# A cross-attention kernel on one core: the output projection as seven block products, weights divided early, statistics on ScalarE

## The chip, the core and the metric

The kernel runs on one core of a Trainium2 chip. The core's engines work side by side, each through its own queue in order: TensorE (PE in the profile, PEld for its weight loads) multiplies and writes its results to PSUM, eight banks of 512 fp32 columns each; VectorE (DVE), ScalarE (ACT) and GpSimd (POOL) do elementwise work; SyncE (SP) issues the transfers (DMA) between device memory and SBUF. In this kernel only VectorE and ScalarE read PSUM. Times are device microseconds; the kernel's time is the median of several runs.

## The reference

For each of 64 batches, with `x` of 256 rows by 512 and `c` (the context) of 256 rows by 384, all fp32:

```python
text_p  = x @ W_text + b_text           # 256 x 512
audio_p = c @ W_audio + b_audio         # 256 x 512
Q = layer_norm(text_p, g1, beta1)
K = layer_norm(audio_p, g2, beta2)
alpha = softmax(Q @ K.T / sqrt(512))    # 256 x 256
H = (alpha @ audio_p) @ W_out + b_out
out = layer_norm(H + x, g_out, beta_out)
```

## The kernel before

There is one loop over batches `b`, and it is a pipeline over four of them: iteration `b` computes the scores of batch `b`, the context and output products of `b-1` (called `last`), the end of the output of `b-2` (called `done`), q and k of `b+2`, and turns x and c of `b+3`. The order of the work is written out by hand, call by call; the pools say when a buffer comes free, and every engine runs its own calls in the order written.

*q and k* (class `Blocks`). A product of 256 rows by 512 columns is cut in a two by two grid of blocks and computed with seven block products instead of eight (a scheme of Strassen's kind). `sum_x` and `sum_c` form the sums of the turned x and c on GpSimd, `weight_sums` those of the weights, once. `products` writes two of the seven products (256 columns each) to one bank of PSUM, and takes four banks in all; `leave(n)` adds product n into the rows on VectorE, so there are seven such steps for each of q and k: three of 512 columns (1, 6 and 7, where one product is broadcast to both halves) and four of 256. For c, with three chunks of 128 in the contraction, it takes 11 matmuls of 256 columns; for x, with four, 14.

*Norms of q and k.* The weights are centred beforehand, so the mean is zero; `square` sums the squares on ScalarE, `rstd_of` forms the reciprocal root on GpSimd, `normalise` scales on ScalarE. The rows are then stored to device memory (`store`) and read back in another order (`fetch`), `turn` transposes them in blocks of 32 by 32 on VectorE, and `affine` applies gamma and beta on ScalarE. The same way round through memory is taken by the exponentials (`store_e`, `fetch_e`, `turn_e`).

*Attention.* `scores` (8 matmuls of 256 columns), `maxima` on VectorE, `exponentials` on ScalarE with their row sums, `reciprocals` on VectorE. `context` multiplies the turned exponentials with c itself (not with the projected c) and copies the result z to SBUF. W_audio and W_out are folded into one matrix `wao` in the beginning, and both biases into `bao`; `multiply(t)` therefore needs three matmuls of 512 columns for each of two row tiles.

*Output.* `add_bias` adds `bao` to x on GpSimd. `evict(t)` multiplies the product with the reciprocal of the row sum and adds x, on VectorE; then bn_stats and bn_aggr give mean and variance, GpSimd the reciprocal root, and `shift` and `settle` on VectorE apply the norm. The rows go to device memory.

*What sets the order around the change.* PSUM has three pools: four banks in a ring for q and k, two for scores and context, two for the output. On VectorE an iteration begins with `done`'s second eviction, statistics and shift, then `last`'s turned exponentials, then the maxima, and ends with the turn of x and c of `b+3` and `last`'s first eviction. On SP the store of the exponentials stands ahead of the reads of q and k; then come the reads of the exponentials, the loads of x and c and the stores of out, q and k.

Of the kernel before, what the change touches and what calls it, by code (L numbers as in the profile page):

```python
# [9 lines left out]
F32 = mybir.dt.float32  # L10
AF = mybir.ActivationFunctionType
# [11 lines left out]
def kernel(  # L23
# [37 lines left out]

    nc = tc.nc
    ctx.enter_context(tc.manual_schedule())
    B, L, D = x.shape
# [10 lines left out]
    work = ctx.enter_context(tc.tile_pool(name="work", bufs=2))  # L77
    small = ctx.enter_context(tc.tile_pool(name="small", bufs=4))
    scratch = ctx.enter_context(tc.tile_pool(name="scratch", bufs=3, space=bass.MemoryType.DRAM))
    p_pj = ctx.enter_context(tc.tile_pool(name="p_pj", bufs=4, space=PSUM))  # L80
    p_at = ctx.enter_context(tc.tile_pool(name="p_at", bufs=2, space=PSUM))
    p_y = ctx.enter_context(tc.tile_pool(name="p_y", bufs=2, space=PSUM))

    def squares(dst, src):

# [73 lines left out]
    def arrange(dst, rows_sb, chunks, copy):  # L159

        copy(
            dst.rearrange("p k (q i) -> p k q i", q=NQ),
            rows_sb.rearrange("p (q k i) -> p k q i", q=NQ, i=SQ),
        )

    class RowTurn:


        def __init__(self, rows_sb, chunks, name):
            self.rows, self.chunks = rows_sb, chunks  # L170
            tag = "y" if chunks == DC else "kT"
            self.ar = work.tile([P, 2, chunks, P], F32, tag=tag, name=f"{name}r")
            self.T = work.tile([P, chunks, 2 * P], F32, tag=name, name=f"{name}_0")

# [8 lines left out]
    def turn_weights():  # L183

        waT = []
        for k in range(HC):
            if k % 2 == 0:
                half = work.tile([P, 2, DA], F32, tag="zT", name=f"waT_{k}")
            waT.append(half[:, k % 2, :])
            ps = p_at.tile([P, AC, P], F32, tag="at", name="ps_wa")  # L190
            for a in range(AC):
                nc.tensor.transpose(ps[:, a, :], war[:, a, k, :], ident)
            nc.scalar.copy(
                waT[k].rearrange("p (q a i) -> p a q i", q=NQ, i=SQ),
                ps.rearrange("p a (q i) -> p a q i", q=NQ),
            )
        return waT
# [13 lines left out]

    def fold_multiply(a):

        ps = ps_wao[a] = p_y.tile([P, D], F32, tag="y", name="ps_wao")
        for k in range(HC):
            nc.tensor.matmul(
                ps,
                lhsT=waT[k][:, bass.ts(a, P)],
                rhs=wo_sb[:, k, :],
                start=(k == 0),  # L220
                stop=(k == HC - 1),
            )
# [59 lines left out]
        }  # L282
        return {p: [ap[:, k, :] for k in range(n)] for p, ap in ss.items()}

    def sum_c(cT):

        part = lambda i, j: cT[:, j, bass.ts(i, P)]
        s = work.tile([P, 5, P], F32, tag="csum", name="csum")
        add = nc.gpsimd.tensor_tensor
        add(s[:, 0], part(1, 0), part(1, 1), ALU.add)  # L290
        add(s[:, 1], s[:, 0], part(0, 0), ALU.subtract)
        add(s[:, 2:4], cT[:, 0:3:2, :P], cT[:, 0:3:2, P:], ALU.subtract)
        add(s[:, 4], part(0, 1), s[:, 1], ALU.subtract)
        return {
            1: [part(0, 0)], 2: [part(0, 1), part(0, 2)], 4: [part(1, 1), part(1, 2)],
            5: [s[:, 0], part(1, 2)], 6: [s[:, 1]], 7: [s[:, 2]], 3: [s[:, 4], s[:, 3]],
        }

    def rstd_of(var, n):
        ve = small.tile([P, n], F32, tag="ve", name="ve")  # L300
        nc.gpsimd.tensor_scalar(ve, var, EPS, None, ALU.add)  # L301
        r = small.tile([P, n], F32, tag="rstd", name="rstd")
        nc.gpsimd.tensor_tensor(r, ve, nhalf[:, :n], ALU.pow)  # L303
        return [r[:, t : t + 1] for t in range(n)]
# [153 lines left out]
    class Attention:  # L458
# [36 lines left out]
        def reciprocals(self):  # L495
            self.rden = small.tile([P, LT], F32, tag="rden", name="rden")
            nc.vector.reciprocal(self.rden, self.den)

        def store_e(self):
            self.d = scratch.tile([L, S], F32, tag="ed", name=f"ed_{self.b}")  # L500
            nc.sync.dma_start(self.d.rearrange("(t p) s -> p t s", p=P), self.e)
# [21 lines left out]
        def context(self):  # L523
# [3 lines left out]
            for lo in range(0, AC, 2):  # L527
# [10 lines left out]
                        )  # L538
                nc.scalar.copy(self.zT[:, lo : lo + n, :], ps[:, :n, :])

        def start_output(self):
            self.y = work.tile([P, LT, H], F32, tag="y", name=f"y_{self.b}")
            self.mv = small.tile([P, LT, 2], F32, tag="mvy", name="mvy")
            self.ps_y = {}

        def multiply(self, t):
            ps = self.ps_y[t] = p_y.tile([P, D], F32, tag="y", name="ps_y")
            for k in range(AC):
                nc.tensor.matmul(  # L549
                    ps,  # L550
                    lhsT=self.zT[:, k, bass.ts(t, P)],
                    rhs=wao_sb[:, k, :],
                    start=(k == 0),
                    stop=(k == AC - 1),
                )
# [13 lines left out]
            self.r = {lo + t: r for t, r in enumerate(rstd_of(self.mv[:, lo : lo + n, 1], n))}  # L569

        def shift(self, t):
            nc.vector.scalar_tensor_tensor(
                self.y[:, t, :], self.y[:, t, :], self.mv[:, t, 0:1], go_sb, ALU.subtract, ALU.mult
            )

        def settle(self, t):
            nc.vector.scalar_tensor_tensor(  # L577
# [40 lines left out]
    k[0].multiply(1)  # L618
    mean_wa = means(wa_sb, AC, "mwa")
    k[0].evict(0)  # L620
    war = blk.tile([P, AC, HC, P], F32, tag="kq", name="war")
    for a in range(AC):
        arrange(war[:, a], wa_sb[:, a, :], HC, nc.gpsimd.tensor_copy)
    x_turn.tile(0)
    x_turn.tile(1)
    k[0].evict(1)
# [4 lines left out]
    bt_row = bt_sb.rearrange("p (o h) -> p o h", o=1)  # L631
    mean_ba = means(ba_row, 1, "mba")
    centre(wa_sb, mean_wa, AC)
    wa_blocks = weight_sums(wa_sb, 1, "wasum")
    for n, k2 in ((2, 0), (3, 1), (5, 1), (4, 0)):
        wa_blocks[n].append(wa_sb[:, 2, k2 * H2 : (k2 + 1) * H2])
    k[0].normalise()
    k[0].store()
    wo_sb = weight_by_square(w_out, HC, "wo", nc.sync)
# [69 lines left out]
    fold_multiply(2)  # L709
    fold_evict(2)  # L710
    bao_sb = fold_bias(part)
    q[1].normalise()
    q[1].store()
    q[1].fetch()
# [4 lines left out]
    for b in range(B - 2):  # L719
        three = b + 3 < B  # L720
        at = Attention(b)
        at.scores()
        if done:
            done.evict(1)
            done.scales()
            done.shift(0)
        if last:
            last.turn_e()
        at.maxima()
        if done:  # L730
            done.shift(1)
        at.exponentials()
        at.store_e()
        if b:
            q[b + 1].fetch()
            k[b + 1].fetch()
        at.fetch_e()
        if b + 4 < B:
            blocks[b + 4] = load_squares(b + 4)
        rows[b + 1] = load_rows(b + 1)  # L740
        q2 = q[b + 2] = Blocks("q", b + 2, xs.pop(b + 2), wt_blocks, bt_sb)
        q2.products(1, 2)
        q2.leave(1)
        if done:
            done.settle(0)
        q2.products(6, 5)
        q2.leave(6)
        q2.leave(2)
        q2.leave(5)
        q2.products(7, 3)  # L750
        q2.leave(3)
        q2.leave(7)
        q2.products(4)
        q2.leave(4)
        q2.square()
        q[b + 1].turn()
        at.reciprocals()
        if last:
            last.context()
        q[b + 1].affine(g1_sb, be1_sb)  # L760
        if done:
            done.settle(1)
            done.store()
        q2.scales()
        add_bias(b)
        k[b + 1].turn()
        k[b + 1].affine(g2_sb, be2_sb)
        q2.normalise()
        q2.store()
        k2 = k[b + 2] = Blocks("k", b + 2, cs.pop(b + 2), wa_blocks, ba_sb)  # L770
        k2.products(1, 2)
        k2.leave(1)
        k2.products(6, 5)
        k2.leave(6)
        k2.leave(2)
        k2.leave(5)
        k2.products(7, 3)
        k2.leave(3)
        k2.leave(7)
        k2.products(4)  # L780
        k2.leave(4)
        k2.square()
        k2.scales()
        if last:
            last.start_output()
            last.multiply(0)
        if three:
            xT[b + 3] = turn_x(b + 3)
            xs[b + 3] = sum_x(xT.pop(b + 3))
            cT[b + 3] = turn_c(b + 3)  # L790
            cs[b + 3] = sum_c(cT.pop(b + 3))
        k2.normalise()
        k2.store()
        if last:
            last.evict(0)
            last.multiply(1)
        done, last = last, at


# [2 lines left out]
    k[B - 1].fetch()  # L802
    rows[B - 1] = load_rows(B - 1)
    at.scores()
    done.evict(1)
    done.scales()
    last.turn_e()
    at.maxima()
    at.exponentials()
    add_bias(B - 2)  # L810
    last.context()
    at.reciprocals()
    q[B - 1].turn()
    last.start_output()
    last.multiply(0)
    q[B - 1].affine(g1_sb, be1_sb)
    at.transpose_e()
    at.copy_e()
    done.finish()
    done.store()  # L820
    last.evict(0)
    last.multiply(1)
    k[B - 1].turn()
    k[B - 1].affine(g2_sb, be2_sb)
    add_bias(B - 1)
    at.context()
    last.evict(1)
    last.scales()
    end = Attention(B - 1)
    end.scores(end=True)  # L830
    at.start_output()
    at.multiply(0)
    end.maxima()
    end.exponentials()
    end.reciprocals()
# [50 lines left out]
```

## Time and profile before

| what | us |
|---|---|
| median of 3 runs | 1449.62 (1448.57 to 1450.06) |
| the profiled execution's own time | 1451.83 |
| its span, first to last instruction | 1450.0 |
| TensorE busy | 1429.6 (99%) |
| VectorE busy | 1223.8 (84%) |
| ScalarE busy | 731.0 (50%) |
| GpSimd busy | 699.0 (48%) |
| DMA engines, mean busy share | about 0.8 |

Busy time is a share of the whole span, and an engine with less than the most of it can still set the time for a stretch. A group of the profile is read as: line, engine, operation, output and inputs, shape and count, then busy time and the mean of one in ns, then the idle time just before it and what ended it. A matmul shows as two records of its kind. The chain that ended last is followed back from the end through whatever released each step.

### The profile page before, as it was taken

To read this page: it belongs to the slowest core of one execution; us is meant where nothing else is said; L and a number is where in the kernel's file an instruction comes from. 1 tells how busy PE (TensorE), PEld (TensorE's weight loads), DVE (VectorE), ACT (ScalarE), POOL (GpSimd) and SP (SyncE) were. 2 spreads that over 40 slices of the span, in tenths; PEclk is the share of its full clock that TensorE was granted. 3 is DMA by queue.
4 is the path that set the end of the run, shared out by engine and by line. 5 is a ranking of instruction groups with operands and counts; after the bars stand their busy time and mean duration, and the time that the engine had idled before them with its cause. 6 is when DMAs were issued, how large, how long until landed. Compare 5 with 4: busy or idle time off the path is not lost.

```text
span 1450.0 us, 20424 instructions
## 1 busy us (share of the span) xinstructions
PE 1429.6 (99%) x5799; PEld 1098.4 (76%) x5799; DVE 1223.8 (84%) x2061; ACT 731.0 (50%) x1689; POOL 699.0 (48%) x1041
## 2 busy tenths in 40 slices
PE   7999999999999999999999999999999999999997
PEld 4777787787787787787777777877877877877874
DVE  5669988888888888888888889888888888888876
ACT  4545554554544544545545545545545445455452
POOL 5445545544545444455445445445444544454442
PEclk9999999999999999999999999999999999999999
DMA  9678878887877978887888878778778788878872
GB/s 206 171 226 248 244 209 245 234 217 229 246 209 229 236 211 237 217 237 229 222 233 235 216 232 242 210 231 246 200 237 228 223 229 224 230 229 233 222 205 89
DMA packets 450275, 322.41 MB, mean 222 GB/s; under 512 B 154740, under 2 KB 382580, under 8 KB 450164
## 3 DMA queue, kind: packets, MB, share of 16 engines
q1 hardware_dynamic: 450164, 321.11, 79.4%
q8 instruction: 47, 0.77, 0.2%
q14 instruction: 64, 0.52, 0.1%
HBM read 204.09 MB, written 116.92 MB: 221 GB/s over the span
## 4 chain that ended last, share of the span: by engine, by line
PE 92%; DMA 4%; DVE 1%; SPq 1%; issue 1%; POOL 0%; ACT 0%; POOLq 0%; DVEq 0%
PE ps_q L431 25%; PE ps_y L549 22%; PE ps_k L431 20%; PE ps_sc L470 15%; PE ps_z L532 11%; DMA qd<-qr 1%; DMA cq<-in_ctx_dram 1%; SPq L88 1%; DMA wt<-in_L_xattn_W_text_dram 1%; DMA ed<-e 0%; DMA wo<-in_L_xattn_W_out_dram 0%; DVE kr L442 0%; DVE qr L442 0%; DMA kq<-kd 0%; DVE y L577 0%
## 5 line engine op out<-in xcount | busy, mean ns | idle before, releaser
L301 POOL TENSOR_SCALAR ve<-var 128x2 f32<-128x2 f32 x126 | 27.7, 220 | 675.0 <-ACT junk L339 674.9
L549 PE MATMUL ps_y<-wao,zT 128*128 128x512 f32 x768 | 340.3, 592 | 0.0
L549 PEld LDWEIGHTS ps_y<-wao,zT 128*128 128x128 f32 x768 | 145.8, 190 | 156.1 <-issue 139.2
L470 PEld LDWEIGHTS ps_sc<-kT,qT 128*128 128x128 f32 x1024 | 193.9, 190 | 54.9 <-issue 21.0
L470 PE MATMUL ps_sc<-kT,qT 128*128 128x256 f32 x1024 | 232.0, 380 | 0.6 <-ACT kT L405 0.6
L442 DVE TENSOR_TENSOR qr<-ps_q,qr 128x512 f32<-128x512 f32 x378 | 188.2, 512 | 48.6 <-PE ps_q L431 36.6
L339 ACT ACTIVATE junk<-qr 128x512 f32<-128x512 f32 x126 | 79.4, 630 | 271.5 <-DVE qr L442 271.5
L442 DVE TENSOR_TENSOR kr<-ps_k,kr 128x512 f32<-128x512 f32 x378 | 188.3, 512 | 27.2 <-PE ps_k L431 4.9
L487 ACT ACTIVATE e<-ps_sc,nmx 128x256 f32<-128x256 f32 x128 | 59.4, 469 | 282.5 <-DVE nmx L480 282.5
L532 PE MATMUL ps_z<-eT,c 128*128 128x256 f32 x768 | 176.6, 379 | 0.8 <-ACT eT L521 0.7
L431 PE MATMUL ps_q<-wtsum,xsum 128*128 128x256 f32 x756 | 173.7, 379 | 0.9 <-POOL xsum L276 0.9
L605 POOL TENSOR_TENSOR x<-x,bao 128x512 f32<-128x512 f32 x128 | 171.7, 1362 | 4.0 <-DMA x<-in_x_dram 4.0
L431 PE MATMUL ps_k<-wa,cT 128*128 128x256 f32 x630 | 166.9, 379 | 0.1
L532 PEld LDWEIGHTS ps_z<-eT,c 128*128 128x128 f32 x768 | 145.8, 190 | 21.6 <-ACT eT L521 0.9
L431 PEld LDWEIGHTS ps_q<-wtsum,xsum 128*128 128x128 f32 x756 | 143.5, 190 | 21.1 <-POOL xsum L276 1.7
L303 POOL TENSOR_TENSOR rstd<-ve,nhalf 128x2 f32<-128x2 f32 (+1 forms) x193 | 141.8, 734 | 16.0
L405 ACT ACTIVATE kT<-kT,columns 128x256 f32<-128x256 f32 x256 | 132.4, 588 | 12.7 <-DVE kT L398 10.1
L405 ACT ACTIVATE qT<-qT,columns 128x256 f32<-128x256 f32 x256 | 132.9, 591 | 11.6 <-DVE qT L91 11.5
L431 PEld LDWEIGHTS ps_k<-wa,cT 128*128 128x128 f32 x630 | 119.5, 190 | 16.6 <-PE ps_z L532 0.4
L367 ACT ACTIVATE kr<-kr,rstd 128x512 f32<-128x512 f32 x126 | 84.1, 714 | 74.8 <-POOL rstd L303 74.8
L431 PE MATMUL ps_q<-wt,xT 128*128 128x256 f32 x504 | 119.2, 379 | 0.7 <-DVE xT L91 0.7
L577 DVE SCALAR_TENSOR_TENSOR y<-y,rstd,beo 128x512 f32<-128x512 f32 x128 | 103.6, 810 | 4.9 <-POOL rstd L303 4.6
(113 smaller groups left out, 2204.9 us busy)
## 6 DMA issues: line engine op xcount, KB each, us to landing
x<-in_x_dram SPq DMA_DIRECT2D x64, 512.0 KB, 4.7
kd<-kr SPq DMA_DIRECT2D x64, 512.0 KB, 4.6
kq<-kd SPq DMA_DIRECT2D x256, 128.0 KB, 3.4
qd<-qr SPq DMA_DIRECT2D x64, 512.0 KB, 7.3
qq<-qd SPq DMA_DIRECT2D x256, 128.0 KB, 2.8
xq<-in_x_dram SPq DMA_DIRECT2D x252, 128.0 KB, 2.8
out_dram<-y SPq DMA_DIRECT2D x63, 512.0 KB, 6.4
cq<-in_ctx_dram SPq DMA_DIRECT2D x252, 96.0 KB, 2.5
```

What stands on the lines that cost most here:

```text
L303: nc.gpsimd.tensor_tensor(r, ve, nhalf[:, :n], ALU.pow)
L339: nc.scalar.activation(junk, self.rows[:, t, :], AF.Square, scale=1.0 / math.sqrt(H), accum_out=self.var[:, t : t + 1],)
L367: nc.scalar.mul(row, row, self.r[t])
L405: nc.scalar.activation(self.T[:, k, :], self.T[:, k, :], AF.Identity, bias=bet[:, k : k + 1], scale=gam[:, k : k + 1],)
L431: nc.tensor.matmul(bank[:, j, :], lhsT=side, rhs=w, start=(i == 0), stop=(i == len(pairs) - 1))
L442: add = lambda o, i0, i1: nc.vector.tensor_tensor(o, i0, i1, ALU.add)
L470: nc.tensor.matmul(self.sc[:, t, :], lhsT=self.qT[:, k, bass.ts(t, P)], rhs=self.kT[:, k, :], start=(k == 0), stop=(k == HC - 1),)
L487: nc.scalar.activation(self.e[:, t, :], self.sc[:, t, :], AF.Exp, bias=self.nmx[:, t : t + 1], accum_out=self.den[:, t : t + 1],)
L532: nc.tensor.matmul(ps[:, j, :], lhsT=self.c_sb[:, s, bass.ts(lo + j, P)], rhs=self.eT[:, s, :], start=(s == 0), stop=(s == ST - 1),)
L549: nc.tensor.matmul(ps, lhsT=self.zT[:, k, bass.ts(t, P)], rhs=wao_sb[:, k, :], start=(k == 0), stop=(k == AC - 1),)
L577: nc.vector.scalar_tensor_tensor(self.y[:, t, :], self.y[:, t, :], self.r[t], beo_sb, ALU.mult, ALU.add)
L605: nc.gpsimd.tensor_tensor(xb[:, t, :], xb[:, t, :], bao_sb, ALU.add)
```

## The change

- The output projection of `last` becomes `Blocks` as well: `sum_c(zT)` on GpSimd forms the sums of z (tile `zsum`), `weights_of_three` those of `wao`, once; its seven products are multiplied at the end of the iteration. Leaves 1, 6, 2 and 5 follow in that iteration, 3, 7 and 4 in the next, after the scores. The rows begin with `bao`.
- A block product mixes rows, so the division by the row sum can no longer be done at the end: `divide_e` multiplies the exponentials with the reciprocals on ScalarE before they are stored.
- x is added by `add_x` on GpSimd, in place of `add_bias` (the last two batches keep `add_bias` and the old output).
- `statistics` replaces bn_stats and bn_aggr: on ScalarE, one pass over each row tile for minus the mean, one for the sum of squares around it.
- q, k and the output share one ring of six PSUM banks.
- The order changes: turn and sums of x and c for `b+3` now follow the scores; the reads of q and k stand ahead of the store of the exponentials, which waits for the division, and the loads of the squares of x and c stand ahead of the reads of the exponentials; `reciprocals` follows q's first leave; both shifts and both settles stand between q's turn and k's products.
- In the start, the rearranged copy of W_audio lies in other buffers.

```diff
-    p_pj = ctx.enter_context(tc.tile_pool(name="p_pj", bufs=4, space=PSUM))
+    p_pj = ctx.enter_context(tc.tile_pool(name="p_pj", bufs=6, space=PSUM))
     p_at = ctx.enter_context(tc.tile_pool(name="p_at", bufs=2, space=PSUM))
-    p_y = ctx.enter_context(tc.tile_pool(name="p_y", bufs=2, space=PSUM))
...
+    def weights_of_three(w_sb, name):
+        ws = weight_sums(w_sb, 1, name)
+        for n, k2 in ((2, 0), (3, 1), (5, 1), (4, 0)):
+            ws[n].append(w_sb[:, 2, k2 * H2 : (k2 + 1) * H2])
+        return ws
...
+        def divide_e(self):
+            for t in range(LT):
+                nc.scalar.mul(self.e[:, t, :], self.e[:, t, :], self.rden[:, t : t + 1])
...
+        def start_products(self):
+            self.o = Blocks("y", self.b, sum_c(self.zT, "zsum"), wao_blocks, bao_sb)
+            self.y = self.o.rows
+        def add_x(self):
+            for t in range(LT):
+                nc.gpsimd.tensor_tensor(self.y[:, t, :], self.y[:, t, :], self.xb[:, t, :], ALU.add)
+        def statistics(self):
+            self.nm = small.tile([P, LT], F32, tag="nm", name="nm")
+            self.ssq = small.tile([P, LT], F32, tag="ssq", name="ssq")
+            for t in range(LT):
...
+                nc.scalar.activation(
+                    junk, self.y[:, t, :], AF.Identity, scale=-1.0 / D, accum_out=self.nm[:, t : t + 1]
+                )
+            for t in range(LT):
...
+                nc.scalar.activation(
+                    junk,
+                    self.y[:, t, :],
+                    AF.Square,
+                    bias=self.nm[:, t : t + 1],
+                    accum_out=self.ssq[:, t : t + 1],
+                )
+            self.r = dict(enumerate(rstd_of(self.ssq, LT, total=True)))
...
         at.scores()
         if done:
-            done.evict(1)
-            done.scales()
-            done.shift(0)
+            done.o.leave(3)
+            done.o.leave(7)
+            done.o.leave(4)
+            done.add_x()
         if last:
             last.turn_e()
+        if three:
+            xT[b + 3] = turn_x(b + 3)
+            xs[b + 3] = sum_x(xT.pop(b + 3))
+            cT[b + 3] = turn_c(b + 3)
+            cs[b + 3] = sum_c(cT.pop(b + 3))
         at.maxima()
-        if done:
-            done.shift(1)
         at.exponentials()
-        at.store_e()
+        q2 = q[b + 2] = Blocks("q", b + 2, xs.pop(b + 2), wt_blocks, bt_sb)
+        q2.products(1, 2)
+        q2.leave(1)
+        at.reciprocals()
+        at.divide_e()
         if b:
             q[b + 1].fetch()
             k[b + 1].fetch()
-        at.fetch_e()
+        at.store_e()
         if b + 4 < B:
             blocks[b + 4] = load_squares(b + 4)
+        at.fetch_e()
         rows[b + 1] = load_rows(b + 1)
...
         if done:
-            done.settle(0)
+            done.statistics()
...
         q2.square()
+        q2.scales()
         q[b + 1].turn()
-        at.reciprocals()
+        if done:
+            done.shift(0)
+            done.shift(1)
         if last:
             last.context()
         q[b + 1].affine(g1_sb, be1_sb)
+        k[b + 1].turn()
+        k[b + 1].affine(g2_sb, be2_sb)
         if done:
+            done.settle(0)
             done.settle(1)
             done.store()
-        q2.scales()
-        add_bias(b)
-        k[b + 1].turn()
-        k[b + 1].affine(g2_sb, be2_sb)
         q2.normalise()
         q2.store()
+        if last:
+            last.start_products()
...
-        if last:
-            last.start_output()
-            last.multiply(0)
-        if three:
-            xT[b + 3] = turn_x(b + 3)
-            xs[b + 3] = sum_x(xT.pop(b + 3))
-            cT[b + 3] = turn_c(b + 3)
-            cs[b + 3] = sum_c(cT.pop(b + 3))
         k2.normalise()
         k2.store()
         if last:
-            last.evict(0)
-            last.multiply(1)
+            last.o.products(1, 2)
+            last.o.leave(1)
+            last.o.products(6, 5)
+            last.o.leave(6)
+            last.o.leave(2)
+            last.o.leave(5)
+            last.o.products(7, 3)
+            last.o.products(4)
```

In the ending, batch 61's output is `Blocks` too, its products after the transposition of batch 62's exponentials; batch 60's `statistics` follow the context of 61 and batch 61's follow the last scores; `end` and `at` keep `multiply` and `evict`.

## The prediction

> **What bounds the kernel now.** I read the page's engine shares first, then the chain that ended last, then the costliest groups with shapes kept apart, one line's durations, the DMA issues, and the timeline of two iterations from 616 us on.
>
> The page (busy time, and the chain by engine):
>
> ```profile
> PE 1429.6 (99%) x5799; PEld 1098.4 (76%) x5799; DVE 1223.8 (84%) x2061; ACT 731.0 (50%) x1689; POOL 699.0 (48%) x1041
> ...
> PE 92%; DMA 4%; DVE 1%; SPq 1%; issue 1%; POOL 0%; ACT 0%; POOLq 0%; DVEq 0%
> ```
>
> The chain in the middle (start, length, what):
>
> ```profile
> 616.97 3.45 PE ps_sc L470 x16
> 620.42 6.04 PE ps_q L431 x28
> 626.47 2.59 PE ps_z L532 x12
> 629.05 4.75 PE ps_k L431 x22
> 633.80 5.15 PE ps_y L549 x12
> 638.95 3.45 PE ps_sc L470 x16
> ```
>
> The chain is TensorE alone and has no gap: one iteration (one batch) is 3.45+6.04+2.59+4.75+5.15 = 21.98 us, and in the stretch 200 to 1380 us TensorE is busy in all of it, at a granted clock of 1.00. So a saving on TensorE counts 1:1 as long as no other engine needs more than the new period. A matmul leaves two records (12 for the six y matmuls). A 256-column record costs 215.8 ns (4.75/22), a 512-column one 429.2 ns (5.15/12).
>
> The groups that give my prices (mean ns after the comma), and one line's min/median/max:
>
> ```profile
> L577 DVE SCALAR_TENSOR_TENSOR y<-y,rstd,beo 128x512 f32<-128x512 f32 x128 | 103.6, 810 | 4.9 <-POOL rstd L303 4.6
> ...
> L442 DVE TENSOR_TENSOR kr<-ps_k,kr 128x256 f32<-128x256 f32 x252 | 101.2, 422 | 15.2
> ...
> L558 DVE SCALAR_TENSOR_TENSOR y<-ps_y,rden,x 128x512 f32<-128x512 f32 x128 | 93.1, 728 | 16.3 <-PE ps_y L549 15.6
> L238 DVE BATCH_NORM_STATS2 st<-y 128x6 f32<-128x512 f32 x128 | 88.9, 695 | 4.4
> L442 DVE TENSOR_TENSOR kr<-ps_k,kr 128x512 f32<-128x512 f32 x126 | 87.2, 692 | 12.0 <-PE ps_k L431 4.9
> ...
> L398 DVE STREAM_TRANSPOSE kT<-kq 128x512 f32<-128x512 f32 x124 | 80.8, 689 | 24.0 <-DMA kq<-kd 20.8 <-issue 3.2
> ```
> ```profile
> L577 DVE SCALAR_TENSOR_TENSOR y<-y,rstd,beo x128: 727/743/1846, 99.2 to 1446.2; 128x512 f32<-128x512 f32 x128
> ```
>
> VectorE is the second load: in one period (597.99 to 619.98) it is busy 19.1 us, ScalarE 11.4, GpSimd 11.0; it also waits at times for a DMA (kT). These issues matter later (KB each, median us to landing):
>
> ```profile
> kd<-kr SPq DMA_DIRECT2D x64, 512.0 KB, 4.6
> kq<-kd SPq DMA_DIRECT2D x256, 128.0 KB, 3.4
> qd<-qr SPq DMA_DIRECT2D x64, 512.0 KB, 7.3
> ```
>
> **TensorE.** The six 512-column matmuls of the output become 11 of 256 columns (the shape of k's products): 22 x 215.8 ns = 4.75 us for 5.15, so -0.405 us, and a period of 21.58. In the loop the products stand 61 times: 61 x 0.405 = -24.7 us, and once in the ending: -0.4.
> Against it speaks the Trainium skill ("TensorE: Matmul & The Clock Gate", Back-to-back issue gap): in a stream of weight loads and matmuls the spacing is set by both, so ten more loads per iteration would not be free. A load here is 190 ns; exposed, ten cost +1.9 us and the time would be 1450 - 25 + 116 = 1541. The row decides: k's 22 records carry one load each and still follow at 215.8 ns, so the loads fit beneath. I take -0.405.
>
> **VectorE.** Out go two evictions, two bn_stats, two aggregations; in come seven leaves (three of 512, four of 256). Rows overlap slightly, so I price by spacing from start to start on the timeline: eviction 0.75, bn_stats 0.73, aggregation 0.1, together 3.15; seven leaves 3.75 (0.7, 2 x 0.73, 4 x 0.39). Net +0.6. The rest per iteration: q and k leaves 7.5, transposes 5.05 (eT 0.63, xT 1.16, cT 0.86, qT 1.17, kT 1.23), maxima 0.6, shifts and settles 2.85. In all 19.8 us of 21.58.
> Now the order, from the scores' start as 0, each piece waiting for the later of its input and the queue. The seven leaves of k end at 19.6; the output's first four follow to 21.8, its last three (3, 7, 4) to 1.75 of the next iteration; eT, xT, cT to 4.4; maxima 5.0; leave 1 of q 5.65. There the reciprocal is a new wait: it needs both exponentials of ScalarE, 1.85 after the maxima's start (timeline: 664.43 to 666.3), so 6.25; behind it are six leaves of q. But leave 6 needs TensorE's second pair, ready at 7.15. So VectorE meets TensorE with 0.85 us to spare; then q's leaves end at 10.4, qT 11.6, shifts 13.0, kT 14.2, settles 15.7, k's leaves 19.6 again. Nothing of the net +0.6 reaches the end while that 0.85 lasts; without it each further 0.1 us is 6.1 us of time. Where VectorE is late, TensorE is not stopped at once: with six banks in the ring, output bank (7,3) is the one k's (1,2) filled, free at 17.4 and wanted at 19.4.
>
> **The shared port.** The Trainium skill ("SBUF — State Buffer", Who interferes with whom) calls the second port pair of VectorE and GpSimd an exclusive lock for the whole instruction; VectorE takes it with two SBUF inputs. Shift and settle are such, and the change puts four GpSimd sums near the settles. By that rule four operations could each be blocked for a GpSimd instruction (0.45 to 1.04 us, say 0.75): +3.0 us, period 23.7, and 1450 + 61 x 1.7 = 1554. The row shows a lock (median 743, worst 1846) but a mean of only 810, with the bias additions of 1.36 us beside it then. I take +0.07 each, +0.3 in all, and leave 0.55 us spare.
>
> **ScalarE.** Added: two divisions (0.52 apart, as the affine steps of that width) 1.05; four passes at 0.74 apart (k's squares, 0.62 each plus the accumulator read): 2.95. Load 11.4 + 4.0 = 15.4 of 21.58. In order: exponentials to 6.1, divisions (wait for the reciprocal) 7.5, statistics 10.5 (wait for x on GpSimd, done at 4.4), q's squares 12.0, copies of z 12.9 (z ends at 12.1), affine q and k 17.1 (wanted by the scores at 21.58: 4 us of cover), q's scaling 18.3, k's squares 20.3, k's scaling 22.7. Against before k's store comes about 1 us later; what is late next is k's way through DRAM (below). Without the 4 us, TensorE would wait.
>
> **GpSimd.** The bias addition goes, x's addition comes: equal, 2.7. Four sums of z are new: 0.45+0.58+1.04+0.45 = 2.5 (csum's rows). 11.0 + 2.5 = 13.5 of 21.58. The queue: x 1.8 to 4.4, sums of x and c to 9.7, the statistics' rstd (waits for ScalarE, 10.5; q's rstd, the z sums and k's rstd stand behind it) 11.5, q's 13.0, z's sums 13.0 to 15.6. TensorE wants them at 18.1: 2.5 us of cover. The earlier turn of the next x and c needs transfers issued before 16 of the iteration before: landed.
>
> **SP.** Every iteration issues the same 26 transfers. e's store moves from 5.4 to about 7.9, since it waits for the divisions; behind it stand cq and xq (8), e's four reads, x, c, out, q's and k's stores. q's and k's reads now go ahead of it. e's reads are issued by 14.1 and land by 17.5 (3.3 us); wanted at 25: hidden.
>
> **Start and end.** The second and third iterations take 24.15 and 23.87 (scores start at 63.13, 87.28, 111.15), 4.05 us over the steady one, partly in a wait for the sums of x, which now come ten us earlier. I take -2.5, between -4 (all) and 0. In the ending GpSimd's queue is x, bias, the statistics' rstd, then z's sums; the rstd waits for four passes that ScalarE begins only after its copies of z. Those end at 6.9 after the scores' start (timeline of before: 1415.2 against 1408.3), the passes at 9.9, rstd 10.9, the second sum 11.9, where TensorE has finished pair (1,2) at 8.2: +3.6 us (0 to 4.5), with no cover, since TensorE has no gap there before.
>
> **Sum.** -24.7 - 0.4 - 2.5 + 3.6 = -24.0. The profiled execution took 1451.83 (span 1450.0 and 1.8 around it), so it would take 1427.8; the median shown is 2.2 lower: 1449.62 - 24.0 = 1425.6.
>
> **Rivals.**
> TensorE stays gapless (as above): 1425.6, with start and end at their bounds 1420.5 to 1429. For it: every cover worked out is positive, and the new ring is longer (6 banks for 4). Chance 0.72.
> VectorE's order sets the period, between 21.58 and 21.98: contention and the reciprocal take more than 0.85. For it: 19.8 + 0.3 + 0.55 of bubble is 96% of the period; against: TensorE's lead of 2 us absorbs single delays. At 21.8 the loop gains 11: 1449.6 - 11 + 0.7 = 1439 (1429 to 1447). Chance 0.12.
> Slower: k's way through DRAM becomes the cycle. From k's last leave to its store 3.33 (679.25 to 682.58), landing 4.6, four reads of which the last starts 1.4 later, landing 3.4, kT 1.23, the two settles now between kT and k's leaves 1.44, k's leaves 3.77: 19.2 us, against 21.58. For it: kT waited for this transfer 39 times already, and the settles are new in the cycle; against: k's reads no longer stand behind e's store. If the two landings take 2.4 us more than their medians it sets the period, from 2.8 us more it is slower than before; at 3.2 more (as the longest kq, 6.6), 22.4: 1449.6 + 25 + 1 = 1476. Chance 0.13.
> No change: the 22 records cost what 12 did, or start and end eat the gain: 1449 to 1452. Chance 0.03.
>
> **How the numbers follow.** A measurement here tells about 0.2% (2.9 us) from no change. Faster: 0.72 + 0.12 = 0.84; within 0.2%: 0.03; slower 0.13. The range goes from the likeliest's lower bound to the middle of the second case: 1420 to 1441, leaving out 0.13 slower, 0.03 and a third of 0.12.
>
> **What would show it.** Right: y's group of 22 records of 256 columns, 4.75 us in the chain; scores 21.58 us apart; no gap on TensorE from the fifth iteration on; VectorE waiting for q's second pair (leave 6); z's sums done 2 us before their products; one gap of 3 to 4 us in the ending before pair (6,5). Wrong: kT waiting for its transfer in most iterations with gaps before the scores or output pairs; settles well above 0.81 us; VectorE without any wait for TensorE.

## The result and the profile after

The changed kernel takes 1429.74 us (1427.52 to 1430.98, 4 runs) against 1449.71 us: a ratio of 0.9862 (95% interval 0.9845 to 0.9879), 20 us less. The forecast was 1425.6 us, 4.1 us lower.

The page of the changed kernel, busy time of each engine and the chain by engine:

```profile
PE 1406.8 (98%) x6419; PEld 1219.1 (85%) x6419; DVE 1270.3 (89%) x2123; ACT 937.5 (66%) x2309; POOL 874.7 (61%) x1293
...
PE 96%; DVE 1%; DMA 1%; POOL 0%; ACT 0%; SPq 0%; issue 0%; POOLq 0%; DVEq 0%
```

The three engines beside TensorE all got more work, and TensorE less: 1406.8 for 1429.6 us. The chain in the middle of the changed kernel (start, length, what):

```profile
690.32 3.45 PE ps_sc L481 x16
693.77 6.04 PE ps_q L442 x28
699.82 2.59 PE ps_z L547 x12
702.40 4.75 PE ps_k L442 x22
707.15 4.75 PE ps_y L442 x22
711.90 3.45 PE ps_sc L481 x16
```

TensorE is still alone in it and without a gap. Only the output's line differs from before: 22 records in 4.75 us where 12 took 5.15. The scores now follow each other after 21.58 us, for 21.98. The spans, cut at the starts of the scores:

| stretch | before, us | after, us | difference |
|---|---|---|---|
| start to the first scores | 48.81 | 49.63 | +0.82 |
| first iteration | 14.33 | 14.32 | 0 |
| second and third | 48.02 | 43.45 | -4.57 |
| the 59 that follow | 1297.11 | 1273.41 | -23.70 |
| from the last but one scores to the end | 41.74 | 48.37 | +6.63 |
| span | 1450.0 | 1429.2 | -20.8 |

Two things are to be explained: why VectorE's, ScalarE's and GpSimd's new work cost nothing in the loop, and why the ending lost 6.6 us where the forecast had a net 3.2 (3.6 less 0.4). TensorE's timeline in that ending of the changed kernel (in brackets the idle time before, and what ended it):

```profile
1387.24 0.60 PE L530 MATMUL ps_e<-ident,e 128*128 128x128 f32 x4
1387.68 1.46 PE L442 MATMUL ps_y<-wao,zT 128*128 128x256 f32 x6
1392.52 2.07 PE L442 MATMUL ps_y<-waosum,zsum 128*128 128x256 f32 x4 [3.38 <-POOL zsum L291]
1394.39 1.06 PE L442 MATMUL ps_y<-wao,zT 128*128 128x256 f32 x2
1395.24 1.06 PE L442 MATMUL ps_y<-waosum,zsum 128*128 128x256 f32 x2
```

The gap before pair (6,5) is there, ended by the second sum of z as forecast: 3.5 us from start to start beyond a record's own time. But behind it two records stand 0.85 us apart, where two normally take 0.43: TensorE runs at half speed. The same trace by stretches (us, TensorE busy with its records, granted clock, DMA share, GB/s):

```profile
1388.45:1391.86 3.41, 0.69 (x4) 1.00 0.99 293
1391.86:1395.28 3.42, 2.76 (x7) 0.50 0.08 30
1395.28:1398.69 3.41, 3.41 (x10) 0.50 0.00 0
```

TensorE works some 6.2 us of this at a clock of 0.50, which costs it about 3.0 us.

### The profile page after: what moved, and what is told of

The parts are those of the page before. It is cut to its first block, busy times and chain, and to the rows that moved or that the text cites. A ratio compares the mean times of both kernels' runs of the same rounds, so it can differ in the third digit from the quotient of the medians.

```text
span 1429.2 us, 23268 instructions
## 1 busy us (share of the span) xinstructions
PE 1406.8 (98%) x6419; PEld 1219.1 (85%) x6419; DVE 1270.3 (89%) x2123; ACT 937.5 (66%) x2309; POOL 874.7 (61%) x1293
## 4 chain that ended last, share of the span: by engine, by line
PE 96%; DVE 1%; DMA 1%; POOL 0%; ACT 0%; SPq 0%; issue 0%; POOLq 0%; DVEq 0%
PE ps_q L442 27%; PE ps_k L442 21%; PE ps_y L442 21%; PE ps_sc L481 15%; PE ps_z L547 11%; DMA wt<-in_L_xattn_W_text_dram 1%; PE ps_wao L216 1%; PE ps_q L332 0%; DVE yr L627 0%; DVE yr L618 0%; DVE y L602 0%; DVE st L238 0%; DMA out_dram<-yr 0%; DVE y L627 0%; POOL ve L312 0%
## 5 line engine op out<-in xcount | busy, mean ns | idle before, releaser
L312 POOL TENSOR_SCALAR ve<-var 128x2 f32<-128x2 f32 x126 | 44.9, 356 | 304.1 <-ACT junk L350 304.1
L453 DVE TENSOR_TENSOR kr<-ps_k,kr 128x512 f32<-128x512 f32 x378 | 188.1, 511 | 24.3 <-PE ps_k L442 0.5
L453 DVE TENSOR_TENSOR yr<-ps_y,yr 128x512 f32<-128x512 f32 x372 | 185.1, 511 | 27.5 <-PE ps_y L442 3.8
L563 POOL TENSOR_TENSOR yr<-yr,x 128x512 f32<-128x512 f32 x124 | 156.9, 1275 | 62.9 <-DVE yr L453 62.9
L314 POOL TENSOR_TENSOR rstd<-ve,nhalf 128x2 f32<-128x2 f32 (+1 forms) x193 | 158.6, 822 | 16.1
L442 PE MATMUL ps_y<-wao,zT 128*128 128x256 f32 x620 | 164.7, 380 | 0.0
L350 ACT ACTIVATE junk<-kr 128x512 f32<-128x512 f32 x126 | 79.4, 630 | 98.0 <-DVE kr L453 98.0
L442 PEld LDWEIGHTS ps_y<-wao,zT 128*128 128x128 f32 x620 | 118.2, 191 | 16.2
L627 DVE SCALAR_TENSOR_TENSOR yr<-yr,rstd,beo 128x512 f32<-128x512 f32 x124 | 128.3, 1071 | 0.3
```

Source lines behind the costliest of these rows:

```text
L350: nc.scalar.activation(junk, self.rows[:, t, :], AF.Square, scale=1.0 / math.sqrt(H), accum_out=self.var[:, t : t + 1],)
L442: nc.tensor.matmul(bank[:, j, :], lhsT=side, rhs=w, start=(i == 0), stop=(i == len(pairs) - 1))
L453: add = lambda o, i0, i1: nc.vector.tensor_tensor(o, i0, i1, ALU.add)
L563: nc.gpsimd.tensor_tensor(self.y[:, t, :], self.y[:, t, :], self.xb[:, t, :], ALU.add)
L627: nc.vector.scalar_tensor_tensor(self.y[:, t, :], self.y[:, t, :], self.r[t], beo_sb, ALU.mult, ALU.add)
```

## The experiments

The theory: TensorE sets the loop, VectorE has a few tenths of a us to spare in it, and the ending's loss is the wait for the sums of z plus a half clock that this wait brings about. Rivals: the half clock is a chance of its own; VectorE has no room, or plenty; the ring and the order of the transfers do not matter.

**The changed kernel again.** No edit.

> The changed kernel once more, unchanged, so that the others have it beside them: 1429.7 (1427.5 to 1431.0 so far). If the slow stretch in the ending (granted clock 0.50 from 1392.5 to 1398.7 us in its profile) depends on the gap of 3.5 us before it, it should be there again whenever the gap is; if it was a chance of that one execution, this profile has the gap and a clock of 1.00 behind it.

1429.0 us (1427.88 to 1430.67). Its profile has the gap, with the same 3.39 us of idle time, and the clock stays at 1.00:

```profile
1386.69:1390.10 3.41, 1.70 (x10) 1.00 1.01 245
1390.10:1393.51 3.41, 1.73 (x8) 1.00 0.39 144
1393.51:1396.93 3.42, 3.42 (x18) 1.00 0.00 0
```

So the half clock does not follow every such gap. The distance between the last two scores tells how much of it an execution has: 17.86 us here, 20.88 in the first profile of the same kernel, and 19.54 and 20.69 in two other versions below that keep the gap.

The traces show what decides. Within one profile the half clocks begin whole multiples of 3.413 us apart: with the output in banks of its own (below) at 87.56, 258.23, 428.90 and 575.67 us, which is 50, 50 and 43 times that. The stretches above are cut on this grid. In the first profile the gap falls mostly into one of them, 2.72 us of it; here it is halved, 1.7 us in each of two. In the thirteen profiles, from 60 us on, all 36 stretches of full clock with 2.00 us or more of idle time were followed by the half clock, and none of the others, which reach 1.94 us. Before the end of the kernel the half clock lasted into a second stretch where the first was itself idle for 0.66 us or more, and ended where that was at most 0.55.

**The sums of z first in the ending.**

```diff
     last.context()
+    last.start_products()
     done.statistics()
     at.reciprocals()
     q[B - 1].turn()
-    last.start_products()
```

> In the ending the sums of z are queued on GpSimd ahead of the statistics' reciprocal root of batch 60 instead of behind it. The prediction's step for the ending: the second sum is then ready at about 8.1 us after the scores' start, where TensorE ends pair (1,2) at 8.2, so the gap of 3.5 us goes, and if the half clock comes from the gap the 3.1 us of slow records go with it: 1429.7 - 6.6 = 1423. If the slow stretch has another cause: 1426. If something else in the ending holds the time (VectorE's or ScalarE's queue): above 1427.

1425.8 us (1424.8 to 1426.18), 3.2 less than the unchanged version beside it. The gap before pair (6,5) is gone, the clock is 1.00, and the last two scores are 14.82 us apart. The expected 6.6 did not all come. Part of it had supposed that every execution drops; and the ending is still 43.45 us long, for 41.74 before the change. One new wait is small (0.5 us from start to start before z of batch 62, for the copy of the turned exponentials, which stands behind the statistics on ScalarE and is no longer hidden by the gap); the other is VectorE's, the matter of the last experiment.

**TensorE kept busy in the gap.**

```diff
     last.o.products(1, 2)
+    warm = p_at.tile([P, 2 * P], F32, tag="at", name="ps_warm")
+    for i in range(8):
+        nc.tensor.matmul(warm, lhsT=ident, rhs=wo_sb[:, 0, : 2 * P], start=True, stop=True)
     last.o.leave(1)
```

> The gap is kept in the data (the order is that of the changed kernel) but TensorE is kept busy in it: eight matmuls of 256 columns whose result nobody reads, 16 records x 215.8 ns = 3.45 us, between pair (1,2) and pair (6,5). If the idle time itself brings the half clock: pair (6,5) still starts about 8.4 us after pair (1,2)'s start or so, at full clock, and the time is 3.1 us less than that of the changed kernel: 1426.6. If the clock falls for another reason: no less than 1429.7.

1428.07 us (1427.1 to 1428.56): 0.9 less than the unchanged version, not 3.1. Its profile has the last two scores 17.86 us apart and a full clock, exactly as the unchanged version has when the clock does not drop. The size was missed because it supposed that every execution drops. The ranges of the two overlap, so the times alone decide nothing; the clocks do. Of the seven profiles with the gap six dropped at it: three of the four in which the loop keeps its 21.58 us (by 3.0, 2.8 and 1.7 us), and all three of the slower loops further below. Of the four with the changed loop but without the gap (this one and three with the sums first) none did before the last scores. Every execution has its mean granted clock on record, too: of the 14 with the gap and the loop at 21.58 us 8 show 0.995 or 0.996, and of the 18 without the gap none is below 0.997.

**The settles moved behind k's leaves.**

```diff
-        if done:
-            done.settle(0)
-            done.settle(1)
-            done.store()
         q2.normalise()
...
         k2.leave(4)
+        if done:
+            done.settle(0)
+            done.settle(1)
+            done.store()
         k2.square()
```

> Both settles and the store of the output go from before k's leaves to behind them, where GpSimd is idle; nothing else moves. The prediction took 0.07 us each for the shared port; the profile of the changed kernel shows settles of 1.07 us beside the sums of z, against 0.74 alone. If GpSimd's sums are what slows them: settles back to 0.73 to 0.76 us and VectorE waits some 0.5 us more per iteration for TensorE, while the time stays within 2 us of 1429.7, since TensorE has no gap to close. If they are slow for another reason: still near 1.07.

1430.18 us (1429.83 to 1430.69), the same within the scatter. The settles, in the groups by line and shape: first of the changed kernel,

```profile
L627 DVE SCALAR_TENSOR_TENSOR yr<-yr,rstd,beo 128x512 f32<-128x512 f32 x124 | 128.3, 1071 | 0.3
```

then of this version:

```profile
L627 DVE SCALAR_TENSOR_TENSOR yr<-yr,rstd,beo 128x512 f32<-128x512 f32 x124 | 89.1, 759 | 0.3
```

1071 ns beside GpSimd's sums of z, 759 away from them. The time is not in the total, and turns up as VectorE's wait for TensorE, in the waits of both (us in total, times, longest), the changed kernel first:

```profile
DVE qr L453 <- PE ps_q L442: 24.8, 112, 1.0
```
```profile
DVE qr L453 <- PE ps_q L442: 78.4, 168, 1.0
```

That is 53.6 us more; in turn VectorE's wait for the exponentials falls from 32.0 to 7.6 us, so some 0.5 us per iteration are new, as expected.

**A dose of extra work on VectorE, small and large.**

```diff
         k2.products(1, 2)
+        nc.vector.memset(idle, 0.0)     # idle is 128x256; the large dose has four
         k2.leave(1)
```

> VectorE gets one more instruction per iteration, between the settles and k's leaves: a memset of 128x256 in a tile that nobody reads, some 0.3 us (its own duration d is read from the profile). In the changed kernel VectorE waits about 0.41 us per iteration for TensorE after the reciprocal (0.16 before leave 6, 0.25 before leave 3; the 0.49 before the reciprocal is a wait for ScalarE that moves along with VectorE). Theory: 62 iterations x (d - 0.41) if positive, so no change: 1429 within 3, period 21.58. Rival: VectorE has no room at all and the time grows by 62 x d = 18: 1447.

1430.2 us (1429.74 to 1430.66), period 21.58: a memset of 0.27 us per iteration costs nothing measurable. VectorE's waits for q's products fall from 24.8 to 13.5 us.

> Four such memsets per iteration, about 1.1 to 1.2 us. Theory of 0.41 us of room: the period becomes 21.58 + 4d - 0.41, with 4d = 1.15 a period of 22.3 and 1429 + 45 = 1474; waits of VectorE for TensorE gone, TensorE waiting for banks or turned tiles. Rival: TensorE's lead and the reciprocal's wait hide all of it (room above 1.1 us): 1429. Other rival: no room: 1429 + 62 x 1.15 = 1500.

1494.9 us (1493.3 to 1496.4), 1.031 (1.028 to 1.034) of the kernel before. The period is mostly 22.60. VectorE's timeline from the settles on, first of the changed kernel,

```profile
704.26 2.06 DVE L627 SCALAR_TENSOR_TENSOR yr<-yr,rstd,beo 128x512 f32<-128x512 f32 x2
706.24 0.68 DVE L453 TENSOR_TENSOR kr<-ps_k,ba 128x512 f32<-128x512 f32 x1
707.02 3.26 DVE L453 TENSOR_TENSOR kr<-ps_k,kr 128x512 f32<-128x512 f32 x6
```

then with the large dose:

```profile
714.31 2.07 DVE L627 SCALAR_TENSOR_TENSOR yr<-yr,rstd,beo 128x512 f32<-128x512 f32 x2
716.38 1.45 DVE L834 MEMSET idle<- 128x256 f32 x4
717.75 0.63 DVE L453 TENSOR_TENSOR kr<-ps_k,ba 128x512 f32<-128x512 f32 x1
718.48 3.27 DVE L453 TENSOR_TENSOR kr<-ps_k,kr 128x512 f32<-128x512 f32 x6
```

From the settles' start to k's second leave it takes 4.17 us for 2.76. The four memsets cost VectorE 1.41 us, and the period grew by 1.02, so the room was about 0.39 us; it was expected at 0.41. The time was expected at 1474 because four memsets were taken as 1.15 us. Where TensorE feels it, in the waits:

```profile
PE ps_y L442 <- DVE kr L453: 50.3, 60, 1.6
```

That is the output's pair (7,3), held by k's leaves that free the bank of k's pair (1,2): the place to which the prediction gave 2 us of lead.

**The output in banks of its own.** Four banks for q and k, two for the output.

```diff
-    p_pj = ctx.enter_context(tc.tile_pool(name="p_pj", bufs=6, space=PSUM))
+    p_pj = ctx.enter_context(tc.tile_pool(name="p_pj", bufs=4, space=PSUM))
+    p_y = ctx.enter_context(tc.tile_pool(name="p_y", bufs=2, space=PSUM))
...
-            bank = p_pj.tile([P, 2, H2], F32, tag="pj", name=f"ps_{self.name}")
+            pool, tag = (p_y, "y") if self.name == "y" else (p_pj, "pj")
+            bank = pool.tile([P, 2, H2], F32, tag=tag, name=f"ps_{self.name}")
```

> One part undone: four banks in a ring for q and k and two for the output, as before the change, with everything else as changed. The output's pair (7,3) then needs the bank of its own pair (1,2), which leaves 1 and 2 free only about 21.7 us after the scores' start, where TensorE wants it at 19.4. Theory: 2.3 us of wait in each of 61 iterations, period 23.9, 1429 + 140 = 1569. Rival: the six-bank ring does not matter and TensorE finds other room: below 1440.

1604.9 us, from one execution; most periods are 24.12, some near 25. The wait, as expected, is for the output's own leaves:

```profile
PE ps_y L444 <- DVE yr L455: 143.5, 62, 2.7
```

143.5 us in 62 iterations, 2.3 each. With its own two banks the output's block products would have cost 155 us instead of gaining 20: without the shared ring the change does not pay. The periods near 25 are again the half clock. It comes ten times in the loop, each time after a gap of 2.3 to 2.7 us, lasts 3.4 us and lengthens the iterations around it, 16 us in all (TensorE's stretches, as above):

```profile
254.82:258.23 3.41, 1.25 (x6) 1.00 0.42 163
258.23:261.64 3.41, 3.41 (x10) 0.50 0.73 231
261.64:265.06 3.42, 3.42 (x18) 1.00 0.88 225
```

**The store of the exponentials ahead of the reads of q and k.**

```diff
+        at.store_e()
         if b:
             q[b + 1].fetch()
             k[b + 1].fetch()
-        at.store_e()
```

> One part undone: on SP the store of the exponentials stands ahead of the reads of q and k again, with everything else as changed (so it waits for the divisions, and q and k wait behind it). Theory, the prediction's slower rival: the store is ready at 7.8 us after the scores' start, k's last read is issued at about 12 and lands at 15.4, where VectorE wants k's turn at 12.7; as k's leaves, the output's leaves, the maxima and the next store of the exponentials all follow that turn, the cycle is 24.3 us long: 1429 + 61 x 2.7 = 1594, with the turn of k waiting for its transfer in every iteration. Rival: these transfers are hidden in any order: 1429 within 5.

1576.4 us, from one execution, periods mostly 23.85. The price was near (24.3 expected), the place was not: it is q's turn that waits, not k's.

```profile
DVE qT L91 <- DMA qq<-qd: 182.5, 63, 4.0
```

q's turn stands ahead of k's on VectorE and its reads start only once the store is through (SP issues the store at 721.40, q's reads from 721.85 on; VectorE waits for them until 726.95), so k's transfer is hidden behind q's.

**bn_stats back on VectorE.** The body of `statistics` is exchanged, and the shift subtracts its mean again:

```diff
+            self.mv = small.tile([P, LT, 2], F32, tag="mvy", name="mvy")
+            for t in range(LT):
+                moments(self.mv, self.y[:, t, :], t)
+            self.r = dict(enumerate(rstd_of(self.mv[:, :, 1], LT)))
```

> One part undone: the output's statistics are two bn_stats and two aggregations on VectorE again, at the same place in the order, with everything else as changed. That gives VectorE 2 x (0.73 + 0.10) = 1.66 us more per iteration and takes four passes (2.63 us) from ScalarE. Theory of about 0.35 to 0.41 us of room on VectorE (from the two memset runs): period 21.58 + 1.66 - 0.38 = 22.86, 1429 + 62 x 1.28 = 1508, or some 0.3 us less per iteration if the settles meet the sums of z less. Rival: ScalarE's passes were what holds the order, and without them the time stays at 1429.

1484.3 us (1483.7 to 1484.9), 1.023 (1.020 to 1.026) of the kernel before; period 22.51. VectorE's timeline there:

```profile
702.17 0.67 DVE L238 BATCH_NORM_STATS2 st<-yr 128x6 f32<-128x512 f32 x1
...
703.77 3.23 DVE L453 TENSOR_TENSOR qr<-ps_q,qr 128x512 f32<-128x512 f32 x6
...
710.59 1.81 DVE L609 SCALAR_TENSOR_TENSOR yr<-yr,rstd,beo 128x512 f32<-128x512 f32 x2
712.32 0.68 DVE L453 TENSOR_TENSOR kr<-ps_k,ba 128x512 f32<-128x512 f32 x1
713.10 3.26 DVE L453 TENSOR_TENSOR kr<-ps_k,kr 128x512 f32<-128x512 f32 x6
```

VectorE got 1.60 us (702.17 to 703.77). The two settles meet the sums less and give 0.25 back (2.51 us from their start to k's second leave, for 2.76), so it has 1.35 more, and 0.93 of that reached the period: a room of 0.42, about what the memsets show. Without the move of the statistics to ScalarE there is no room for the seven leaves.

**The ending, one step further.** The sums first, as above, and:

```diff
     last.o.leave(5)
+    done.finish()
+    done.store()
     last.o.products(7, 3)
...
     at.context()
-    done.finish()
-    done.store()
```

> The version with the sums of z ahead of the statistics' reciprocal root in the ending, once more and unchanged, as company for the next: 1425.8 (1424.8 to 1426.2 so far).

> As the version beside it, and the shifts and settles of batch 60 in the ending go ahead of the last three leaves of batch 61, so that they no longer run beside GpSimd's additions of 512 columns (there they took 1.58 to 1.76 us each for 0.75 alone, and the eviction of batch 62 then waited 1.05 us for the store behind them). If VectorE's chain is what the ending now hangs on: shifts and settles at 0.75, the wait for the store gone, and 1 to 1.5 us less than the version beside it. If TensorE's end sets it: the same within 0.5 us.

On the same chip the sums-first version, once more, took 1427.36 us (1426.72 to 1429.36) and this one 1425.22 us (1424.95 to 1425.42), 2.1 less. In the two profiles 1.2 us of the difference lie in the stretch from the last but one scores to the end (44.35 and 43.12 us) and most of the rest in the first iterations, which are alike in both. The earlier profile of the sums-first version had 43.45 us in that stretch, so the size of this gain, between 0.3 and 1.2 us, is not settled. VectorE's timeline there, of the sums-first version:

```profile
1396.12 0.74 DVE L618 SCALAR_TENSOR_TENSOR yr<-yr,nm,go 128x512 f32<-128x512 f32 x1
1396.97 1.57 DVE L627 SCALAR_TENSOR_TENSOR yr<-yr,rstd,beo 128x512 f32<-128x512 f32 x1
1398.46 1.76 DVE L618 SCALAR_TENSOR_TENSOR yr<-yr,nm,go 128x512 f32<-128x512 f32 x1
1400.26 1.64 DVE L627 SCALAR_TENSOR_TENSOR yr<-yr,rstd,beo 128x512 f32<-128x512 f32 x1
...
1404.80 0.75 DVE L602 SCALAR_TENSOR_TENSOR y<-ps_y,rden,x 128x512 f32<-128x512 f32 x1 [1.04 <-DMA out_dram<-yr]
```

and of this one:

```profile
1393.15 0.74 DVE L618 SCALAR_TENSOR_TENSOR yr<-yr,nm,go 128x512 f32<-128x512 f32 x1
1394.00 0.75 DVE L627 SCALAR_TENSOR_TENSOR yr<-yr,rstd,beo 128x512 f32<-128x512 f32 x1
1394.66 0.74 DVE L618 SCALAR_TENSOR_TENSOR yr<-yr,nm,go 128x512 f32<-128x512 f32 x1
1395.44 0.75 DVE L627 SCALAR_TENSOR_TENSOR yr<-yr,rstd,beo 128x512 f32<-128x512 f32 x1
```

Beside GpSimd's additions of 512 columns three of these four operations took 1.57 to 1.76 us, away from them 0.75, and the store that the next eviction waited for comes earlier. This version has the lowest ratio, 0.9825 (0.9812 to 0.9839) of the kernel before, but the sums-first version had 0.9829 (0.9816 to 0.9843) in its earlier executions, which is the same within the intervals.

## Why the prediction was right, and where it was off

*TensorE, -0.405 us per iteration.* Held: 4.75 us in the chain, the period 0.40 shorter in each of the 59 steady iterations, no gap in them. The rule about weight loads that was set against it did not show: the added loads fit beneath the matmuls (weight loads busy 85% of the span, for 76%).

*VectorE, 0.85 us to spare, 0.55 with contention.* Right in sign, somewhat too large: the memsets show 0.39 and bn_stats 0.42. The term that was mis-sized is the shared port: the settles were given +0.07 us each by the mean of the row before, and moving them shows 0.31 each (1071 against 759 ns), so a sign that the prediction itself had named as one of being wrong, settles well above 0.81 us, came true while the result held. The rule of the Trainium skill ("SBUF — State Buffer", Who interferes with whom), by which the loser waits for the whole instruction of the other, gave the direction; its +3.0 us per iteration was far too much, the +0.3 taken too little, and 0.6 is measured. With 0.6 the prediction's own sum would leave 0.25; that 0.4 is left means that some other term was too dear by about 0.15, which was not followed.

*The reciprocal as a new wait and leave 6 as the meeting point.* As predicted: VectorE waits 0.49 us for the exponentials in each iteration, then 0.16 and 0.25 for q's pairs.

*ScalarE and GpSimd.* Hidden, as predicted. The GpSimd sums of z end at 16.3 us after the scores' start for 15.6 predicted, wanted at 18.1, so 1.8 us of cover are left of 2.5.

*SP.* The new order was called hidden in a sentence; the undone order shows that it carries 2.3 us per iteration. The rival about k's way through DRAM had the price right for that order and the wrong transfer: q's.

*Start.* -2.5 predicted (0 to -4); the second and third iterations give -4.57, of which 0.8 is the matmul saving, so -3.8. The first scores come 0.8 us later, but that point lies between 47.9 and 49.9 us in the profiles of all versions, and is scatter of the loads at the start.

*Ending.* This is the step that failed in size. The gap was forecast at +3.6 and is 3.5, from the very queue that was named, GpSimd's; the rest was not foreseen. By parts, from the profiles:

| version | last but one to last scores, us | last scores to the end, us | together |
|---|---|---|---|
| before | 14.60 | 27.14 | 41.74 |
| changed, first profile | 20.88 | 27.49 | 48.37 |
| changed, again (no half clock) | 17.86 | 28.17 | 46.03 |
| sums of z first (no gap) | 14.82 | 28.63 | 43.45 |

The gap costs 3.0 us up to the last scores, and the half clock 3.0 more, of which 0.7 are made up by the end, where VectorE leads the chain. About 1 us is added behind the last scores (28.17 for 27.14). VectorE's settles beside GpSimd's additions are a small part of it at most, since with them moved away it is still 28.30; the rest was not followed. Against the forecast of 3.2 the ending lost 4.3 without the half clock and 6.6 with it.

The Trainium skill warns of this ("TensorE: Matmul & The Clock Gate", HAM oscillation: no idle time above some 3.4 us) and says that the clock goes by a window that runs freely (the same page, What's actually happening). The prediction used that page for the loads and not for the gap that it had itself computed. The free window is what the traces show, 3.413 us long; the limit of 3.4 us is not: 2.0 us of idle time within one window were enough, and gaps of 2.3 us brought the half clock.

*The sum.* In the first profile, the loop's 61 iterations gave -24.5 (-24.7 predicted), start and first scores -3.0 (-2.5), the ending +6.6 (+3.2): -20.8 of span for -24.0. In the other profile of the changed kernel the span is 1426.1 us, -23.9, almost the forecast, and that is luck in part: the start gave 1.2 us more than predicted and the ending lost 1.1 us more.

## What to carry to other kernels

Where one engine is gapless, count its columns: here that saving arrived in full, and the question was only whether the next engine's queue, with its contention, still closed within the shorter period; two memset doses on that engine measured the room. What made the work move off the bounding engine free was, beside the arithmetic moved to ScalarE, the places: one ring of banks long enough that late leaves don't stop TensorE, and transfers ordered by when they are ready. A gap on TensorE can cost nearly twice its length (here 3.0 us, and up to 3.0 more by the clock), so a queue on another engine that opens such a gap is worth reordering first. And before a gap is called too short for the clock to fall, see how much of it can lie within one of the clock's windows.

## What the hardware showed that was not expected

After an idle time of 3.4 us TensorE's granted clock fell to 0.50 for 3.4 or 6.8 us in six profiles and not in a seventh (0 to 3.0 us lost). It is not chance but the place of the gap on a grid of 3.413 us: 2.00 us idle within one stretch of the grid always brought the half clock, 1.94 us never did, and so gaps of 2.3 us were enough in a loop. VectorE operations with two SBUF inputs took 0.75 us alone, 1.07 beside GpSimd operations of 128 to 256 columns, and up to 1.76 beside GpSimd additions of 512 columns, which themselves grew (the two additions of the bias took 2.49 us in the ending before VectorE's settles, 3.41 beside them); operations reading PSUM kept their 0.42 and 0.69 us throughout.
